# Layer 0's self attention: row maxima turned in one piece, results regrouped by DMA, the causal mask put down before the scores, and a new order of the places

## The chip, the cores and the metric

The kernel runs on one core of a Trainium2 chip. The time is the device time of one execution in microseconds (us), as the chip's profiler records it. Before the change, three runs took 2233.22, 2234.9 and 2238.18 us; their median is 2234.9 us. One more execution was taken with a full profile, and all durations below are from it. Engines are named as the profile names them: PE is TensorE doing matrix multiplications, PEld its loading of stationary operands, DVE is VectorE, ACT ScalarE, POOL GpSimd and SP SyncE, which here only issues DMAs.

## The reference

A decoder of two layers, with a layer norm behind each addition. Each layer has a self attention, a cross attention and a feed-forward part. The change touches only the first of the six, layer 0's self attention: 4 batches of 1024 positions and 256 channels, 16 heads of 16 channels, with a causal mask.

```python
def attention(x, w_in, b_in, w_out, b_out):          # x: 4 x 1024 x 256
    q, k, v = split(x @ w_in.T + b_in, 3)             # each as 16 heads of 16
    scores = einsum('bhqd,bhkd->bhqk', q / sqrt(16), k)
    scores = scores + where(tril(1024, 1024), 0, -inf)
    attn = softmax(scores, axis=-1)
    out = einsum('bhqk,bhkd->bhqd', attn, v)          # heads side by side: 4 x 1024 x 256
    return out @ w_out.T + b_out

x = layernorm(x + attention(x, ...))
... # cross attention to 154 positions, feed-forward with a convolution, then layer 1
```

The softmax is computed with the row's maximum taken off before the exponential, so each row's maximum must be known before any of its exponentials is taken.

## The kernel before

**Steps.** The self attention runs in 16 steps; step s takes batch s//4 and the four heads 4·(s%4) to 4·(s%4)+3. The four heads lie in four groups of 32 partitions: rows 0 to 15 of a group hold a head's 16 channels, row 16 is an extra one. `projected` (L275 to 289) computes queries and keys of eight heads for 512 positions at once, and `spread` (L293 to 299) moves them with four DMAs per step on SP's queue from 16 adjacent rows into their groups, `qpads` (two buffers) and `kpads` (three). Row 16 of the keys is 1.

**Two passes.** Scores are computed twice. Pass A of a step (`a_unit`) multiplies queries by keys, with queries on the partitions, only to get the row maxima on DVE: `tensor_reduce` L332 for whole blocks, L348 for blocks on the diagonal, to which the mask is first added by a matmul. `highest` (L355) joins a row's partial maxima, negated, into `nmt`, column 16 of each head's 32; `shifted_queries` (L360 to 370) turns `nmt` with eight 128x128 transposes on PE and adds it to the queries, so that row 16 of `qs` holds minus the maximum. Pass B (`b_unit`) multiplies keys by `qs`, keys on the partitions; the row of ones takes the maximum off. ACT takes the exponential (L399) into `p`, POOL zeroes what the mask forbids (L402), and `weighted` (L420 to 439) multiplies `p` with the values and sums in `acc`. The values' tile has 17 columns per head, 16 values and a one, so row 16 of a head's result is its softmax denominator. `normalised` (L441 to 455) turns the results back with eight transposes per step, takes the reciprocal of the denominators, 16 columns at a time (L454), and multiplies (L455). When a batch's four steps are done, `turned_back` (L462 to 470) transposes the normalised results once more (16 transposes per batch), and `out_projected` (L472 to 482) projects 128 positions at a time and adds `x`; the layer norm follows.

**Places.** Each pass of a step has 18 units, so a step has 18 places. At a place, `together` runs one unit of pass A of step s beside one unit of pass B of the step before (L191 is the line of the one helper that issues all these matmuls), the two in opposite pairs of row groups. A unit's product takes two of the seven PSUM banks that rotate among all that is computed here; the eighth is `acc`. Pass B of step s-1 starts two places after the step's border. In the gap between two places stands other work of PE: the products of `weighted` (a whole 512-column piece, or pieces of 384 and 128 that different gaps take), projections of later steps, transposes, output projections.

**Order.** The order of PE's work is written out by hand. Every piece is put down with a time, 20 units to a step (`at(when, ...)`, from L489 on); the pieces are sorted by that time and issued, and PE's instructions and the DMAs so marked keep that order. A piece at `s * T + 1 + j` is the pair of units of place j; pieces at `+0.5` stand in the gap behind the place before. The other engines' order follows from what PE produces.

Of the kernel before, what the change touches and what calls it, by code (L numbers as in the profile page):

```python
# [8 lines left out]
F32 = mybir.dt.float32  # L9
# [20 lines left out]
def decoder_kernel(ctx: ExitStack, tc: tile.TileContext, a: dict, out: bass.AP):  # L30
# [155 lines left out]
    def self_attention(wk, pss, psa):  # L186
# [29 lines left out]
        vts, nmps, nmts = [], [], []  # L216
        for i in range(2):
            vt = wk.tile([P, NC, 17 * H + 16], F32, tag=f"v{i}", name=f"v{i}", bufs=1)
            nc.gpsimd.memset(vt, 1.0)
            vts.append(vt)  # L220
            nmp = wk.tile([P, 4, NC, 3], F32, tag=f"nmp{i}", name=f"nmp{i}", bufs=1)
            nc.gpsimd.memset(nmp, -3.0e38)
            nmps.append(nmp)
            nmt = wk.tile([P, NC, 4, 32], F32, tag=f"nmt{i}", name=f"nmt{i}", bufs=1)
            nc.gpsimd.memset(nmt, 0.0)
            nmts.append(nmt)

        bo2 = wk.tile([P, E], F32, tag="bo2", name="bo2", bufs=1)
        t = bank()
        for e in range(2):  # L230
            mm(t[:, :E], l0a_bv[:, e : e + 1].to_broadcast([P, P]), l0a_wo[:, e, :], e == 0, e == 1)
        nc.vector.tensor_tensor(bo2, t[:, :E], l0a_bo, ALU.add)
# [6 lines left out]
        xTs, ons, sts, qss, pts, accs, ots = {}, {}, {}, {}, {}, {}, {}  # L239
# [18 lines left out]
        def values(b, i):  # L258
            t = bank()
            for j in range(2):  # L260
                c = 2 * i + j
                for e in range(2):
                    mm(
                        t[:, j * E : (j + 1) * E],
                        xTs[b][:, e, c * P : (c + 1) * P],
                        l0a_w[:, e, 2 * E :],
                        e == 0,
                        e == 1,
                    )
            (nc.vector.tensor_copy, nc.scalar.copy)[i % 2](  # L270
                vts[b % 2][:, 2 * i : 2 * i + 2, : 17 * H].rearrange("p c (h r) -> p c h r", r=17)[:, :, :, 0:16],
                t.rearrange("p (c h d) -> p c h d", c=2, h=H),
            )

        def projected(kind, i, q):  # L275
# [4 lines left out]
            t = bank()  # L280
            for e in range(2):
                mm(
                    t,
                    l0a_w[:, e, w0 + h * P : w0 + (h + 1) * P],
                    xTs[b][:, e, q * 512 : (q + 1) * 512],
                    e == 0,
                    e == 1,
                )
            nc.scalar.activation(
                sts[kind, i][:, q * 512 : (q + 1) * 512], t, AF.Identity, bias=bias[:, h : h + 1], scale=scale  # L290
            )

        def spread(kind, s):  # L293
            pads = {"k": kpads, "q": qpads}[kind]
            pad = pads[s % len(pads)]
            st = sts[kind, s // 2]
            for g in range(4):
                r = 64 * (s % 2) + 16 * g
                pe(nc.sync.dma_start(out=pad[32 * g : 32 * g + 16, :], in_=st[r : r + 16, :]))
# [12 lines left out]
        def a_unit(s, u, pair):  # L312

            t = [bank() for _ in range(2)]
# [20 lines left out]
            else:  # L335
                q0 = 4 * (u - 7)
                for j in range(4):
                    cols = slice((q0 + j) * P, (q0 + j + 1) * P)
                    rounds.append([
                        (t[g][:, j * P : (j + 1) * P], qt[rows[g], cols], kt[rows[g], cols], j == 0, False)  # L340
# [3 lines left out]
                def after():  # L344
                    for g in range(2):
                        mm(t[g], ident_bf, cmask4.rearrange("p j n -> p (j n)"), False, True)
# [8 lines left out]
        def highest(s):  # L355
            nc.vector.tensor_reduce(
                nmts[s % 2][:, :, :, 16], nmps[s % 2].rearrange("p g q i -> p q g i"), AX.X, ALU.max, negate=True
            )

        def shifted_queries(s):  # L360
            nmt = nmts[s % 2]
            qs = qss[s] = wk.tile([P, S], F32, tag="qs", name="qs")
            for q in range(2):
                t = bank()
# [1295 lines left out]
```

## Time and profile before

| what | us |
|---|---|
| median of three runs | 2234.9 |
| the profiled execution's own time | 2231.4 |
| its span in the profile | 2229.6 |
| start to the first product of pass B (step 0, pass A alone) | 0 to 69.1 |
| both passes, steps 1 to 15 | 69.1 to 702.7 |
| last step's pass B alone | 702.7 to 740.5 |
| output projection of the last batch, until the next part begins | 740.5 to 761.0 |
| all that follows (the other five parts, not touched) | 761.0 to 2229.6 |

PE is busy 94% of the span, DVE 67%, ACT 50%, POOL 23%; the mean granted clock of TensorE is 0.979 of full speed. In the stretch where both passes run, a step takes 633.6/15 = 42.2 us.

How the lines are to be read. A line of the timeline gives a start, a duration, the engine, the source line, the operation, output<-input by the program's names, the shapes, and x with the number of instructions in the group; brackets hold the idle time ahead of the group and what ended it. Matmuls are pipelined, so a group's duration overlaps with the next group's; what a group costs is the distance from its start to the start of the next one. A line of the groups gives busy time in all and the mean of one in ns, then the idle time ahead and its enders. A line of the windows gives, for one stretch, busy us and number of instructions of PE, PEld, DVE, ACT and POOL, then the granted clock, the share of time that the DMA engines were busy, and GB/s.

### The profile page before, as it was taken

The numbers are of one execution on the slowest core, as the hardware profiler recorded it, in microseconds if no ns is written. First come the engines' busy times: TensorE is split into PE (matmuls) and PEld (weight loads), VectorE is DVE, ScalarE is ACT, GpSimd is POOL, SyncE is SP. The second block draws the span as 40 slices with busy tenths as digits, with TensorE's granted clock in tenths as the row PEclk, the third lists the DMA queues.
The fourth block names the chain that finished last, engine by engine and source line by source line (L and its number), as shares of the span: only waits on it lengthen the run. The fifth ranks groups of instructions, "written<-read, shape, count | busy, mean of one in ns | idle before, by whom it ended". The sixth has DMA issues, their size and how long they took to land.

```text
span 2229.6 us, 39020 instructions
## 1 busy us (share of the span) xinstructions
PE 2100.6 (94%) x14708; PEld 1255.9 (56%) x14708; DVE 1491.3 (67%) x3287; ACT 1119.0 (50%) x2861; POOL 510.4 (23%) x1113
## 2 busy tenths in 40 slices
PE   7999999999999899989899989989999999999996
PEld 4554554555454456556556556656666655565654
DVE  4766667776775556658997888886972465555644
ACT  1455554554555365556666655554543234545444
POOL 1111111111111265445455443000000111111102
PEclk9999999999999999999999999999999999999998
DMA  4101100000000100000000100000000010010101
GB/s 111 39 6 53 37 9 15 11 16 15 6 16 1 39 1 20 1 1 1 1 1 1 34 1 22 1 0 1 1 1 1 2 20 15 15 29 10 29 1 38
DMA packets 24445, 34.85 MB, mean 16 GB/s; under 512 B 5953, under 2 KB 19649, under 8 KB 24257
## 3 DMA queue, kind: packets, MB, share of 16 engines
q1 hardware_dynamic: 22640, 31.20, 6.1%
q8 instruction: 117, 1.92, 0.4%
q10 hardware_dynamic: 1616, 1.16, 0.2%
q14 instruction: 72, 0.58, 0.1%
HBM read 15.56 MB, written 4.19 MB: 9 GB/s over the span
## 4 chain that ended last, share of the span: by engine, by line
PE 71%; DVE 20%; ACT 6%; issue 1%; POOL 1%; DMA 1%; SPq 0%; ACTq 0%; POOLq 0%; DVEq 0%
PE s L191 21%; PE t L590 15%; PE s L1196 10%; PE s L590 8%; PE acc L191 6%; DVE gt L946 4%; PE acc L1196 3%; PE t L774 2%; ACT u L749 2%; DVE nmp L332 2%; DVE x L169 1%; DVE nmx L745 1%; DVE bnst L136 1%; DVE gt L956 1%; DVE ht L932 1%
## 5 line engine op out<-in xcount | busy, mean ns | idle before, releaser
L399 ACT ACTIVATE p<-s 128x512 f32<-128x512 f32 x576 | 312.2, 595 | 291.9 <-PE s L191 283.7
L332 DVE TENSOR_REDUCE nmp<-s 128x1 f32<-128x512 f32 (+3 forms) x640 | 298.6, 522 | 153.8 <-PE s L191 153.0
L191 PE MATMUL s<-qs,kp 32*128 32x512 f32 (+3 forms) x1536 | 347.9, 521 | 0.0
L191 PE MATMUL s<-kp,qp 32*128 32x128 f32 (+3 forms) x2304 | 327.7, 407 | 2.4 <-DMA qp<-sq 2.1
L757 POOL TENSOR_SCALAR p<-u,rs 128x128 f32<-128x128 f32 x512 | 215.9, 441 | 284.8 <-DVE rs L753 185.0
L191 PEld LDWEIGHTS s<-kp,qp 32*128 32x128 f32 x2304 | 165.5, 189 | 136.1 <-ACT p L399 46.2
L402 POOL TENSOR_SCALAR_AFFINE_SELECT p<-p 128x256 f32<-128x256 f32 x256 | 99.6, 407 | 567.8 <-ACT p L399 567.8
L749 ACT ACTIVATE u<-s,nmx 128x154 f32<-128x154 f32 x512 | 192.9, 393 | 46.7 <-DVE nmx L745 30.6
L154 POOL TENSOR_TENSOR rstd<-ve,neghalf 128x4 f32<-128x4 f32 (+1 forms) x56 | 58.6, 1046 | 573.6 <-DVE ve L152 569.2
L191 PE MATMUL acc<-p,v 128*32 128x384 f32 (+3 forms) x2016 | 167.9, 420 | 0.1
L191 PEld LDWEIGHTS s<-qs,kp 32*128 32x128 f32 x1536 | 138.8, 183 | 29.1 <-DVE nmp L332 8.4
L590 PE MATMUL t<-xT,xw 128*128 128x512 f32 x256 | 123.3, 605 | 11.8 <-DVE xT L677 8.4
L1353 DVE TENSOR_REDUCE nmt<-s 128x3 f32<-128x462 f32 (+1 forms) x192 | 99.0, 578 | 45.6 <-PE s L1196 45.6
L745 DVE TENSOR_REDUCE nmx<-s 128x4 f32<-128x616 f32 x128 | 100.9, 788 | 39.5 <-PE s L590 38.2
L590 PE MATMUL t<-v,pt 128*128 128x256 f32 x512 | 116.5, 380 | 8.2 <-DVE pt L1105 8.2
L590 PE MATMUL t<-xw,ot 128*128 128x256 f32 x512 | 119.0, 387 | 2.7 <-ACT qt L731 2.6
L946 DVE SCALAR_TENSOR_TENSOR gt<-ht,cw,gt 128x256 f32<-128x256 f32 x256 | 116.4, 500 | 6.5 <-ACT gt L942 5.3
L590 PEld LDWEIGHTS s<-kt,qt 64*128 64x128 f32 x1024 | 75.9, 186 | 72.2 <-issue 50.8
L590 PE MATMUL s<-qt,xT 128*128 128x512 f32 x256 | 115.1, 592 | 0.0
L590 PEld LDWEIGHTS t<-v,pt 128*128 128x128 f32 x512 | 95.8, 190 | 30.5 <-DVE pt L1105 9.8
L348 DVE TENSOR_REDUCE nmp<-s 128x4 f32<-128x512 f32 x128 | 82.4, 686 | 44.8 <-PE s L191 44.4
L749 ACT ACTIVATION_READ_ACCUMULATOR u<-s,nmx 128x1 f32 x512 | 106.4, 208 | 0.0
(259 smaller groups left out, 3851.0 us busy)
## 6 DMA issues: line engine op xcount, KB each, us to landing
qp<-sq SPq DMA_DIRECT2D x128, 64.0 KB, 2.3
kp<-sk SPq DMA_DIRECT2D x64, 64.0 KB, 2.3
out_dram<-x SPq DMA_DIRECT2D x8, 512.0 KB, 2.9
x<-in_x_dram SPq DMA_DIRECT2D x3, 1024.0 KB, 6.5
wf<-in_L_ffn_w_dram SPq DMA_DIRECT2D x2, 1024.0 KB, 6.0
xw<-in_L_xattn_wk_dram SPq DMA_DIRECT2D x1, 1024.0 KB, 6.5
xw<-in_L_xattn_wq_dram SPq DMA_DIRECT2D x1, 1024.0 KB, 5.0
xw<-in_L_xattn_wv_dram SPq DMA_DIRECT2D x1, 1024.0 KB, 5.0
```

The costliest lines, as they stand in the source:

```text
L191: pe(nc.tensor.matmul(o, l, r, start=start, stop=stop))
L332: nc.vector.tensor_reduce(nmp[:, 2 * pair + g, qc, i : i + 1], t[g][:, c0 : c0 + n], AX.X, ALU.max)
L348: nc.vector.tensor_reduce(nmp[:, 2 * pair + g, q0 : q0 + 4, 0], t[g].rearrange("p (j n) -> p j n", j=4), AX.X, ALU.max,)
L399: nc.scalar.activation(p[:, g, :], t[g], AF.Exp)
L402: nc.gpsimd.affine_select(out=v, in_=v, compare_op=ALU.is_ge, fill=0.0, base=0, pattern=[[0, 2], [1, P]], channel_multiplier=-1,)
L590: pe(nc.tensor.matmul(o, l, r, start=start, stop=stop))
L745: nc.vector.tensor_reduce(nmx.rearrange("p i g -> p g i"), t, AX.X, ALU.max, negate=True)
L749: nc.scalar.activation(u[:, 2 * i + g, :], t[:, g, i, :], AF.Exp, bias=nmx[:, i, g : g + 1], accum_out=ssum[:, i, g : g + 1],)
L757: nc.gpsimd.tensor_scalar(p[:, h * P : (h + 1) * P], u[:, h, :P], rs[:, h : h + 1], 1.0, ALU.mult, ALU.mult)
L946: nc.vector.scalar_tensor_tensor(g, ht[:, i, k : k + N], cw[:, hc, k : k + 1], g, ALU.mult, ALU.add)
L1196: pe(nc.tensor.matmul(o, l, r, start=start, stop=stop))
L1353: nc.vector.tensor_reduce(nmts[s % 2][:, 3 * u : 3 * u + n, g, 17], ts[g][:, : n * LK].rearrange("p (c k) -> p c k", k=LK), AX.X, ALU.max, ...
```

## The change

**Maxima.** `highest` leaves the maxima as 128 positions by 32 columns (four heads by eight chunks). `maxima_turned` turns them by a single transpose into 32x128, ACT copies that out of PSUM, and four DMAs put the rows into row 16 of `qs`. `qs` itself is a copy of the queries, made by one DMA of 512 KB (`second_queries`) earlier in the step. The eight transposes and the two additions of `shifted_queries` are gone.

**Results.** The values' tile has 48 columns for a pair of heads: the values of one, 16 ones, the values of the other. A product of 32 columns then yields 16 rows of results and 16 rows that all hold the denominator. `gathered` moves both, with eight DMAs of 64 KB per step, into `on` (results, already in the form that the output projection reads) and `den` (denominators, in the same places). `divided` takes the reciprocal of `den` on DVE, all 128x128 elements of a chunk, eight chunks per pair of steps, and multiplies on POOL. The transposes of `normalised` and of `turned_back` are gone.

**Mask.** For a diagonal unit the mask is now multiplied into the bank first (`causal_mask`, start of the sum), in the gap ahead of the unit, and the scores are added to it. The diagonal units move from places 0 to 3 to places 1, 3, 5 and 7; `a_order` and `b_order` keep the two passes in opposite row groups.

**Order.** Pass B starts four places after the border, not two. Each piece of `weighted` is issued whole, in every second gap, except one piece of 256 columns, with the two of another unit beside it. Projections are made in quarters of 256 positions and values one chunk at a time. The first spread of queries is issued on ACT's queue; the bias of the output projection is computed later, not ahead of everything. For the last batch, half of its last step's results are gathered on their own and the output projection of the first four chunks is placed in the last step.

```diff
-    vt = wk.tile([P, NC, 17 * H + 16], F32, tag=f"v{i}", name=f"v{i}", bufs=1)
+    vt = wk.tile([P, NC, 24 * H], F32, tag=f"v{i}", name=f"v{i}", bufs=1)
...
+T = 20
+DELAY = 4
+
+def gap(s, j):
+    return (s + j // 18) * T + 1.5 + j % 18
...
+def values(b, c):
+    t = bank()[:, :E]
+    for e in range(2):
+        mm(t, xTs[b][:, e, c * P : (c + 1) * P], l0a_w[:, e, 2 * E :], e == 0, e == 1)
+    (nc.vector.tensor_copy, nc.scalar.copy)[c % 2](
+        vts[b % 2][:, c, :].rearrange("p (h r d) -> p h r d", r=3, d=16)[:, :, 0:3:2, :],
+        t.rearrange("p (h r d) -> p h r d", r=2, d=16),
     )
...
-    t = bank()
+    t = bank()[:, :256]
+    cols = slice(q * 256, (q + 1) * 256)
...
+    queue = nc.scalar if (kind, s) == ("q", 0) else nc.sync
     for g in range(4):
         r = 64 * (s % 2) + 16 * g
-        pe(nc.sync.dma_start(out=pad[32 * g : 32 * g + 16, :], in_=st[r : r + 16, :]))
+        pe(queue.dma_start(out=pad[32 * g : 32 * g + 16, :], in_=st[r : r + 16, :]))
+
+def second_queries(s):
+    qs = qss[s] = wk.tile([P, S], F32, tag="qs", name="qs")
+    pe(nc.sync.dma_start(out=qs, in_=qpads[s % 2]))
...
+diagonal = {1: (7, 0), 3: (7, 1), 5: (8, 0), 7: (8, 1)}
+b_order = [divmod((j - DELAY) % 18, 2) for j in range(18)]
+b_order = [(i, 1 - pair if i in (8, 1) else pair) for i, pair in b_order]
+others = [iter((4, 5, 6, 0, 1, 2, 3)) for _ in range(2)]
+a_order = []
+for j, (_, pair) in enumerate(b_order):
+    a_order.append(diagonal[j] if j in diagonal else (next(others[1 - pair]), 1 - pair))
+
+def causal_mask(s, j):
+    t = masks[s, j] = [bank() for _ in range(2)]
+    for g in range(2):
+        mm(t[g], ident_bf, cmask4.rearrange("p j n -> p (j n)"), True, False)
+
+def a_unit(s, j):
+    u, pair = a_order[j]
+    t = masks.pop((s, j)) if j in diagonal else [bank() for _ in range(2)]
...
             rounds.append([
-                (t[g][:, j * P : (j + 1) * P], qt[rows[g], cols], kt[rows[g], cols], j == 0, False)
+                (t[g][:, c * P : (c + 1) * P], qt[rows[g], cols], kt[rows[g], cols], False, c == 3)
...
-            for g in range(2):
-                mm(t[g], ident_bf, cmask4.rearrange("p j n -> p (j n)"), False, True)
...
-def shifted_queries(s):
...
+    hm = hms[s] = wk.tile([P, 4, NC], F32, tag="hm", name="hm")
+    nc.vector.tensor_reduce(hm, nmps[s % 2], AX.X, ALU.max, negate=True)
+
+def maxima_turned(s):
+    t = bank()[:32, :P]
+    pe(nc.tensor.transpose(t, hms[s].rearrange("p g c -> p (g c)"), ident))
+    rows = wk.tile([32, P], F32, tag="mrow", name="mrow")
+    nc.scalar.copy(rows, t)
+    for g in range(4):
+        pe(nc.sync.dma_start(
+            out=qss[s][32 * g + 16 : 32 * g + 17, :].rearrange("p (c n) -> p c n", c=NC),
+            in_=rows[NC * g : NC * g + NC, :],
+        ))
...
+            v0 = 24 * (4 * t4 + g) - 8 * (g % 2)
-                vts[b % 2][:, kc, 17 * (4 * t4 + g) : 17 * (4 * t4 + g) + 32],
+                vts[b % 2][:, kc, v0 : v0 + 32],
...
-def normalised(s, i):
...
-    t = bank()
-    for j in range(4):
-        c = c0 + j
-        pe(nc.tensor.transpose(t[:, j * P : (j + 1) * P], ot[:, c * P : (c + 1) * P], ident))
...
-    rs = small.tile([P, 4, 4], F32, tag="rs8", name="rs8", bufs=2)
-    nc.vector.reciprocal(rs, v[:, :, :, 16])
...
-def turned_back(b, e, q):
...
+def gathered(s, c0=0, n=S, queue=None):
     b, t4 = divmod(s, 4)
+    e = t4 // 2
+    if t4 == 0:
+        ons[b] = wk.tile([P, 2, S], F32, tag="on", name="on")
+    if t4 % 2 == 0:
+        dens[b, e] = wk.tile([P, S], F32, tag="den", name="den", bufs=1)
+    cols = slice(c0, c0 + n)
+    for g in range(4):
+        r = 64 * (t4 % 2) + 16 * g
+        up = 32 * g + 16 * (g % 2)
+        down = 32 * g + 16 * (1 - g % 2)
+        pe(nc.sync.dma_start(out=ons[b][r : r + 16, e, cols], in_=ots[s][up : up + 16, cols]))
+        pe((queue or nc.sync).dma_start(out=dens[b, e][r : r + 16, cols], in_=ots[s][down : down + 16, cols]))
+
+def divided(b, e, c0, n):
+    cols = slice(c0, c0 + n)
+    den, on = dens[b, e][:, cols], ons[b][:, e, cols]
+    nc.vector.reciprocal(den, den)
+    nc.gpsimd.tensor_tensor(on, on, den, ALU.mult)
...
-        mm(t, onT[:, e, c * P : (c + 1) * P], l0a_wo[:, e, :], e == 0, e == 1)
+        mm(t, ons[b][:, e, c * P : (c + 1) * P], l0a_wo[:, e, :], e == 0, e == 1)
...
+at(gap(0, 9), output_bias)
...
+    s0 = 4 * b
+    for q in range(2):
+        for e in range(2):
+            at(gap(s0 - 2, 2 * q) + 0.1 * e if b else -60 + 2 * q + e, x_transposed, b, e, q)
+    places = [(s0 - 1, 14), (s0 - 1, 16), (s0, 0), (s0, 2), (s0, 4), (s0, 14), (s0, 16), (s0 + 1, 0)]
+    if b == 0:
+        places[:2] = [(0, 1), (0, 3)]
+    for c, (s, j) in zip((0, 1, 3, 2, 6, 4, 5, 7), places):
+        at(gap(s, j), values, b, c)
+    places = [(s0 + 5, 14), (s0 + 5, 16), (s0 + 6, 4), (s0 + 6, 14), (s0 + 6, 16), (s0 + 7, 0), (s0 + 7, 2), (s0 + 7, 4)]
+    if b == NB - 1:
+        places[:4] = [(s0 + 4, j) for j in (14, 15, 16, 17)]
+    for c, (s, j) in enumerate(places):
+        at(gap(s, j), out_projected, b, c)
+    for e in range(2):
+        if (b, e) == (NB - 1, 1):
+            for q in range(2):
+                at(gap(s0 + 4, 12.2) if q == 0 else gap(s0 + 5, 5.5), divided, b, e, 512 * q, 512)
         else:
+            for c in range(NC):
+                at(gap(s0 + 2 * e + 3, 9.2 + c), divided, b, e, P * c, P)
...
+    for q in range(4):
+        for kind in "kq":
+            if i == 0:
+                at(-57 + q + 0.1 * (kind == "q"), projected, kind, i, q)
+            else:
+                at(gap(2 * i - (2 if kind == "k" else 1), 6 + 2 * q), projected, kind, i, q)
...
+            at(gap(s - 1, 13.1 if j == 0 else 4.1), spread, "k", s)
+            at(gap(s - 1, 13.2 if j == 0 else 2.1), spread, "q", s)
...
-    at((s + 1) * T + 1.4, shifted_queries, s)
+    at(gap(s + 1, 0) - 0.1, maxima_turned, s)
+    at(gap(s, 4.3), second_queries, s)
...
+    for i in range(9):
+        g = gap(s + 1, 2 * i + 3 + DELAY)
+        for qh, kc, c0 in b_sets[i]:
+            if (i, qh) == (2, 1):
+                continue
+            n = width(qh, kc)
+            last = (i, qh) == (2, 0) or (i, kc) == (8, 7)
+            at(g, weighted, s, qh, i, [(kc, c0, 512 - n, n)], i in (0, 3), last)
+        if i == 3:
+            at(g, weighted, s, 1, 2, [(6, 256, 256, 256)])
+    if s < 4 * NB - 1:
+        at(gap(s + 2, 5.3), gathered, s)
+    else:
+        at(gap(s + 1, 11.2), gathered, s, 0, 512, nc.scalar)
+        at(gap(s + 2, 5.3), gathered, s, 512, 512, nc.scalar)
+    for j in diagonal:
+        at(gap(s, j - 1) + 0.3, causal_mask, s, j)
...
-            units.append((a_unit, s, (7, 8, 0, 1, 2, 3, 4, 5, 6)[j // 2], 1 - j % 2))
-
+            units.append((a_unit, s, j))
+        sb = s - 1 if j >= DELAY else s - 2
         if 0 <= sb < 4 * NB:
-            units.append((b_unit, sb, jb // 2, jb % 2))
+            units.append((b_unit, sb, *b_order[j]))
```

## The prediction

> **What bounds the kernel now.** I read the page's busy shares first, then windows by stage, then PE's timeline over one step with DVE's beside it, then the groups by form, and last the DMA issues. The stages (PE, PEld, DVE, ACT, POOL, clock, DMA share, GB/s), from the windows:
>
> ```profile
> 0.00:69.10 69.10, 52.29 (x272) 32.85 (x272) 36.91 (x76) 7.75 (x11) 7.22 (x16) 0.87 0.36 93
> 69.10:702.70 633.60, 628.47 (x6145) 324.34 (x6144) 439.22 (x952) 336.64 (x615) 96.76 (x241) 1.00 0.09 19
> 702.70:740.50 37.80, 34.76 (x294) 15.40 (x292) 12.91 (x36) 22.53 (x43) 8.78 (x21) 1.00 0.01 2
> 740.50:761.00 20.50, 12.16 (x72) 10.69 (x72) 17.24 (x55) 2.70 (x6) 6.67 (x9) 0.93 0.30 103
> ```
>
> In the 633.6 us with both passes PE is busy 628.5, DVE 439. Two kinds of time are inside PE's: work, and waits too short to show, because a matmul in flight counts as busy. PE's timeline (start, duration) prices the work and shows such waits:
>
> ```profile
> 374.88 1.06 PE L191 MATMUL acc<-p,v 128*32 128x512 f32 x8
> ...
> 382.03 1.98 PE L191 MATMUL s<-xT,qkv 128*128 128x512 f32 x4
> 383.94 0.70 PE L191 MATMUL s<-kp,qp 32*128 32x512 f32 x2
> ...
> 386.90 1.13 PE L191 MATMUL s<-wo,onT 128*128 128x256 f32 x4
> 387.96 0.64 PE L191 MATMUL acc<-p,v 128*32 128x256 f32 x8
> 388.53 0.70 PE L191 MATMUL s<-kp,qp 32*128 32x512 f32 x2
> ...
> 406.55 1.07 PE L366 MATMUL s<-ident,nmt 128*128 128x128 f32 x8 [0.52 <-DVE nmt L356]
> 407.45 0.60 PE L451 MATMUL s<-ident,ot 128*128 128x128 f32 x4
> 407.99 0.38 PE L191 MATMUL s<-kp,qp 32*128 32x128 f32 x2
> ...
> 416.85 0.66 PE L451 MATMUL s<-ident,ot 128*128 128x128 f32 x4
> 417.44 0.70 PE L191 MATMUL s<-kp,qp 32*128 32x512 f32 x2
> ...
> 418.10 1.30 PE L191 MATMUL s<-qs,kp 32*128 32x384 f32 x7
> 419.33 0.85 PE L191 MATMUL acc<-p,v 128*32 128x384 f32 x8
> ```
>
> From start to next start: nmt and ot transposes 407.99-406.55 = 1.44 a step, four transposes 0.59, a 512-column projection of two banks 1.91, an output chunk 1.06, a 256-column piece of `acc` 0.57. Equal distances give 1.00, 0.78, 0.36 for 512, 384, 128 columns: 0.143 + 0.2135 per 128. A place's pair of units takes 1.08.
>
> The hidden wait is at 417.44: this pair takes 1.89. Its second half starts at 418.10, where DVE has just (418.22) cleared the two banks of the unit before:
>
> ```profile
> 416.93 1.29 DVE L332 TENSOR_REDUCE nmp<-s 128x1 f32<-128x512 f32 x2 [0.98 <-PE s L191]
> ```
>
> So PE's work sets the pace, but seven banks couple it to DVE: a gap of only 0.59 between two units costs 0.8 of waiting. Some 40 such gaps make about 30 us.
>
> **The change, part by part.** The base is the profiled execution's own time, 2231.4 us (span 2229.6 and 1.8 around it), 3.5 under the median of the three runs.
>
> *1. PE's work, on the path.* Transposes removed from the stretch 69 to 740: 16 of 1.44, 16 of 0.59 (second half of ot) and 12 of 0.59 (turned back, three batches), 39.5. Added: 16 turns of the maxima at 0.27, worked out as a quarter of 1.07; bounds 0.11 (one transpose's distance in 407.45 to 407.99, with the rest hidden) and 0.59 (a group of four), so 2 to 9 us in all; 4.3. Pieces of `acc` fall from 206 to 143: 63 starts of 0.143, -9. Projections in quarters: 52 of 1.06 for 26 of 1.91, +5.5; values one by one, 24 for 12 in the same way, +3; four output chunks come over from the tail, +4.2; the 64 mask products stay, at distances of 0.44 to 0.53, of which I take about a third at the lower one instead of the higher, -2. Together -35.2-9+10.7, taken as -34.
>
> *2. Bank waits.* Now 30. Afterwards the alternate gaps hold one piece of at least 1.06, and at places 8, 10, 12, 14, 16 the second half of pass B takes the banks that the preceding unit's reductions free 0.08+1.29 = 1.37 after its end: 0.31 of wait each, 0.5 behind a split unit, 1.74 a step, 28; some 5 for the other places. +3 net. Bounds: none of these waits is left (-30), or each is the 0.8 seen at 417.44 (rival C).
>
> *3. The reciprocals: DVE, in front of the reductions that PE waits for.* `divided` puts eight 128x128 reciprocals into the step behind each pair of steps. In the built order they stand on DVE at places 8 to 12 of seven steps: one, then three, three and one between pairs of reductions. No row shows 128 columns. The rows with fewer (groups: busy, mean ns | idle before):
>
> ```profile
> L753 DVE RECIPROCAL rs<-ssum 128x4 f32<-128x4 f32 x128 | 22.1, 173 | 49.6 <-ACT u L749 44.9 <-POOL p L757 2.7 <-issue 1.2
> L857 DVE RECIPROCAL sc<-am 128x8 f32<-128x8 f32 x4 | 0.8, 194 | 0.0
> L454 DVE RECIPROCAL rs<-s 128x16 f32<-128x16 f32 x32 | 7.9, 248 | 10.1 <-PE s L451 10.1
> L332 DVE TENSOR_REDUCE nmp<-s 128x1 f32<-128x128 f32 x128 | 35.9, 280 | 9.8 <-PE s L191 9.8
> ```
>
> A single column takes 162 ns (another group), so an element costs (248-162)/15 = 5.7 ns and 128 columns 248+112x5.7 = 0.89 us. Ends: 0.28, if a long one runs as the reduction of 128; 1.0, by the steepest pair of rows (54 ns for 8 elements). Counted from the end of place 8's unit, with R for one reciprocal: place 9's reductions end at 4.05; three reciprocals and place 10's reductions end at 5.33+3R, which place 11's second half waits for; three more, place 11's reductions, one more and place 12's end at 7.89+7R; place 13 ends 1.08 later, at 8.97+7R in place of 11.2. The loss is 7R-2.2, 4.0 a time and +28 for seven. At R = 0.28 it is 0, at 1.0 33. POOL's multiplication (0.44 for 128x128, 97 of 634 us busy) and the removed additions of L370 (0.68, two a step) and L454/L455 are beside PE.
>
> [...]
>
> *4. Gathering.* SP issues eight more DMAs a step, in program order, behind place 5. Spread DMAs are the nearest:
>
> ```profile
> 437.65 2.41 SPq L299 DMA_DIRECT2D qp<-sq  x4
> qp<-sq SPq DMA_DIRECT2D x128, 64.0 KB, 2.3
> ```
>
> Four of them start within 2.41, 0.63 apart; 2.3 is the landing. From the end of `acc`: ACT's copy 0.75, seven distances of 0.63 up to the last of eight issues 4.4, landing 2.3: 7.45. DVE comes to the first reciprocal at 7.3. So it waits about 0.15, +1 in seven steps; the queue's other entries (spreads, maxima) are places apart. There is no slack (rival B). If the eight go out as slowly as the slowest spread issues, 1.59 apart, it is late by 6.7.
>
> *5. Maxima.* `maxima_turned` is in the place of the transposes, and PE waits for `highest` as now (0.52 at 406.55). Then ACT's copy (0.3, as a 128-column reduction), four issues 2.5, landing 2.3, queue and semaphores: about 8.0 behind pass A's end; pass B's first unit, moved from the second to the fourth place, comes at 10.6. The cover is the four places, 2.6 us; cost 0. The 512 KB copy of the queries is issued 14 places earlier; it lands in 2.9, as the output's 512 KB rows. At worst, rival D.
>
> *6. Ends.* Head: values and the output bias leave the start and queries spread on ACT's queue, so the first unit, at 30.67 behind a DMA, could start at about 26.4; two more places run pass A alone (+2.2), and the start has fewer groups at half clock: -7 (0 to -12). Step 16: the first output chunk at gap 14 needs copy, four issues, landing, a reciprocal of 512 (four of 128: 3.6) and a multiplication, 9.6, of which 4.65 are covered: +5 (3 to 7). Tail: 20.5 becomes 19.7, as DVE's 17.2 of additions and norms there is the limit and only half moves: -1.
>
> Sum: -34+3+28+1+0-7+5-1 = -5, **2226 us**. Against the median, all the same, it would be 2230. With 0.2%, 4.5 us, as the bound of what a measurement tells from no change, it is at the edge of faster.
>
> **The rivals.**
>
> *A: reciprocals as fast as plain operations.* Then R = 0.28, part 3 is 0: 2226-28 = 2198. Against it, the three rows grow steadily with columns. For it, none has more than 16, and start-up may be in the growth.
>
> *B, the slower side: results land late.* The gather's eight issues are the only ones of that length in a row. If they go 1.0 apart (median 0.58, longest 1.59), the last is 3 late and DVE, whose queue is in order, holds the reductions behind the reciprocal; PE stops within two places. 3x7 = 21: 2247. From 1.5 us of lateness on the kernel is slower than before by over 0.2%.
>
> *C: bank waits of 0.8 everywhere.* If a gap of 1.06 gives B no more relief than one of 0.59 does, five places x16x0.8 = 64 for 33: 2257. For it, DVE gains work at exactly those places; against it, pairs behind two-bank gaps of 1.0 now take 1.08.
>
> *D: pass B waits for the maxima's DMAs.* Each us over the 2.6 of cover counts 16 times; one over gives 2242. Against it: it needs 8.0 to become 11.6.
>
> **How the numbers follow.** Main case 0.45, A 0.17, B 0.20, C 0.12, D 0.06. The main case's own range is 2212 to 2238: R between 0.74 and 1.0 (-7, +5), bank waits half or up by a fifth (-10, +6), ends. Over all the range is 2198 to 2251: it goes from the middle of A past B and D, and leaves C's larger half. Faster: half of the main case and all but a little of A, 0.41; same: a third of the main case, 0.14; slower: the rest of it and B, C, D, 0.45.
>
> **What would show it.** Rows of L366, L451's and L467's transposes gone, 16 transposes to 32x128 in their place; `acc` groups 143; first unit of pass A near 26; 128x128 reciprocals of 0.89; at places 10 to 13 of odd steps about 4 us more than in even ones, PE's wait put down to DVE `nmp`. A DVE wait on a DMA of `den` speaks for B, waits of 0.8 in even steps for C, a PE wait on `qs` rows at the fourth place for D. Wrong altogether would be a unit that no longer takes 1.08, or copies into row 16 that slow other transfers.

## The result

The changed kernel is slower: a median of 2252.7 us over five runs (2250.3 to 2261.7) against 2234.9 for the kernel before; the ratio is 1.0086, with a 95% interval of 1.0062 to 1.0109. The forecast was 2226 with a range up to 2251, so its likeliest case lay on the wrong side and the result just outside the range. The profiled execution took 2250.3 us, with a span of 2248.0 against 2229.6.

The windows of the changed kernel, cut at the places that answer to the four windows of before (first product of pass B, end of pass A, last product of `acc`, next part's first copy); columns as before:

```profile
0.00:73.40 73.40, 56.77 (x300) 37.89 (x303) 37.47 (x82) 9.89 (x20) 6.72 (x14) 0.84 0.33 92
73.40:702.00 628.60, 617.09 (x5514) 306.71 (x5513) 455.74 (x949) 333.91 (x644) 122.86 (x296) 1.00 0.20 44
702.00:753.50 51.50, 44.14 (x275) 15.63 (x274) 13.47 (x29) 24.76 (x48) 11.05 (x24) 0.77 0.09 17
753.50:776.60 23.10, 8.52 (x44) 7.07 (x40) 13.90 (x28) 1.37 (x3) 6.19 (x9) 0.71 0.31 103
```

The last step is what stands out: pass B alone took 37.8 us and takes 51.5, at a mean clock of 0.77 where it was 1.00. For all that follows, the two traces and those of the experiments are divided by PE's own events into four stretches: to the turning of step 1's maxima ("head"), from there to the turning of step 15's ("14 steps"), on to the first product of the next part ("last step and tail"), and the rest.

| us | head | 14 steps | last step and tail | rest | span |
|---|---|---|---|---|---|
| before | 104.1 | 601.1 | 56.6 | 1467.9 | 2229.6 |
| after | 104.4 | 599.6 | 73.3 | 1470.7 | 2248.0 |
| difference | +0.3 | -1.5 | +16.7 | +2.8 | +18.4 |

So the bulk of the change, 14 steps with all their transposes, DMAs and reciprocals, came out nearly even, as the sum had it. The time was lost where only pass B runs. PE's timeline there:

```profile
703.00 1.13 PE L191 MATMUL s<-qs,kp 32*128 32x512 f32 x4
...
718.00 1.35 PE L191 MATMUL s<-qs,kp 32*128 32x512 f32 x8
721.16 1.90 PE L191 MATMUL acc<-p,v 128*32 128x512 f32 x16 [1.81 <-ACT ot L447]
722.99 2.08 PE L191 MATMUL s<-qs,kp 32*128 32x512 f32 x4
725.00 1.22 PE L191 MATMUL s<-wo,on 128*128 128x256 f32 x2
730.22 1.22 PE L191 MATMUL s<-wo,on 128*128 128x256 f32 x2 [4.00 <-POOL on L469]
731.38 2.08 PE L191 MATMUL s<-qs,kp 32*128 32x512 f32 x4
733.38 2.08 PE L191 MATMUL s<-wo,on 128*128 128x256 f32 x4
...
763.30 3.99 PE L191 MATMUL s<-wo,on 128*128 128x256 f32 x10 [9.10 <-POOL on L469]
```

Two waits stand in it. At 721.16 `acc` cannot be cleared, because ACT's copy out of it waits: `ot`, the tile that the copy writes, has a single buffer (the kernel before had two), and the gather of step 14 still reads it. At 730.22 the second half of the first output chunk, the channels of the batch's last two steps, waits for its divided results. From 722.1 on the same work also takes almost twice as long: four matmuls of a unit last 2.08, where they lasted 1.13 at 703.00. The clock by windows, and the two long reciprocals on DVE that the output chunks wait behind:

```profile
704.10:722.10 18.00, 15.56 (x155) 6.14 (x157) 0.00 (x0) 15.09 (x30) 6.24 (x16) 1.00 0.18 32
722.10:746.00 23.90, 19.90 (x56) 7.04 (x52) 9.58 (x18) 4.94 (x9) 1.26 (x1) 0.50 0.05 12
746.00:753.50 7.50, 6.58 (x65) 1.94 (x57) 2.95 (x9) 4.13 (x8) 3.54 (x7) 1.00 0.00 0
```

```profile
725.47 3.35 DVE L468 RECIPROCAL den<-den 128x512 f32<-128x512 f32 x1 [22.49 <-DMA den<-ot]
...
758.54 3.35 DVE L468 RECIPROCAL den<-den 128x512 f32<-128x512 f32 x1 [8.33 <-DMA den<-ot]
```

PE is busy 19.9 of the 23.9 us at half clock; half of that, 10 us, is my estimate of the loss. The step's account: 10 for the clock, 1.8 and 4.0 for the two waits, 4 for output chunks that came over from the tail, which makes 20. Against it stand some 3 us of transposes that are gone and some 3 us of batch 2's output chunks (three of them) that now come earlier, so that from the turning of step 15's maxima to the last product of `acc` PE takes 49.4 instead of 35.4. The tail did not get shorter (21.5 before, 24.1 after, from the last product of `acc` on), since its second half now waits 9.1 for gather, reciprocal and multiplication.

### The profile page after: what moved, and what is told of

Read it like the earlier page. It is cut to its first block, busy times and chain, and to the rows that moved or that the text cites. A ratio compares the mean times of both kernels' runs of the same rounds, so it can differ in the third digit from the quotient of the medians.

```text
span 2248.0 us, 38049 instructions
## 1 busy us (share of the span) xinstructions
PE 2101.9 (93%) x14051; PEld 1241.8 (55%) x14052; DVE 1505.7 (67%) x3257; ACT 1119.0 (50%) x2901; POOL 538.6 (24%) x1169
## 4 chain that ended last, share of the span: by engine, by line
PE 66%; DVE 22%; ACT 6%; issue 2%; DMA 1%; SPq 1%; POOL 1%; ACTq 0%; POOLq 0%; DVEq 0%
PE s L191 20%; PE t L598 15%; PE s L1204 10%; PE s L598 7%; PE acc L191 5%; DVE gt L954 4%; PE acc L1204 3%; DVE den L468 2%; DVE nmp L343 2%; ACT u L757 2%; PE t L782 2%; DVE x L169 1%; DVE nmx L753 1%; DVE gt L964 1%; DVE ht L940 1%
## 5 line engine op out<-in xcount | busy, mean ns | idle before, releaser
L191 PE MATMUL s<-qs,kp 32*128 32x512 f32 (+3 forms) x1536 | 372.4, 527 | 8.1 <-DVE nmp L343 8.0
L191 PE MATMUL s<-kp,qp 32*128 32x128 f32 (+3 forms) x2304 | 332.5, 407 | 5.5 <-DMA qp<-sq 5.4
L191 PEld LDWEIGHTS s<-qs,kp 32*128 32x128 f32 x1536 | 151.1, 185 | 55.2 <-DVE nmp L343 34.9
L191 PE MATMUL acc<-p,v 128*32 128x512 f32 (+3 forms) x1536 | 156.1, 499 | 3.4 <-ACT ot L447 1.8
L757 ACT ACTIVATION_READ_ACCUMULATOR u<-s,nmx 128x1 f32 x512 | 106.4, 208 | 0.0
```

The costliest lines, as they stand in the source:

```text
L191: pe(nc.tensor.matmul(o, l, r, start=start, stop=stop))
L757: nc.scalar.activation(u[:, 2 * i + g, :], t[:, g, i, :], AF.Exp, bias=nmx[:, i, g : g + 1], accum_out=ssum[:, i, g : g + 1],)
```

## The experiments

Each single execution carries its own pauses at half clock, so the tables' stretches are compared, not only the time. "Half clock" is how long the clock's record stood at 0.5 in the stretch named. "After" is the changed kernel's profiled execution.

### Four runs on the reciprocals and the last step

Without the short reciprocals:

```diff
-            nc.vector.reciprocal(den, den)
+            if n > P:
+                nc.vector.reciprocal(den, den)
```

> Leaves out the 56 reciprocals of 128x128 (the results are multiplied by the denominators instead); the two of 512 columns stay, and so does every transfer and wait. Theory of the bursts: each of the seven odd steps from 3 to 15 loses 4.0 us to three reciprocals standing between reductions, so these steps become about 4 us shorter, the even ones stay, and the profiled time falls from 2250.3 by 28 to about 2222. Rival (the reciprocals fit beside PE's work, and the steps are long for the bank waits alone): steps 3 to 15 stay within 0.5 us each, the time within 5 us of 2250.

The last batch's output chunks all at the end:

```diff
             if b == NB - 1:
-                places[:4] = [(s0 + 4, j) for j in (14, 15, 16, 17)]
+                places = [(s0 + 6, j) for j in range(NC)]
```

> The last batch's first four output chunks go behind pass B, with the other four; the wait of 4.0 us for them inside the last step is gone, the wait of 1.8 us of acc for the copy out of it (single buffer ot, held by the gather of the step before) stays. Theory W (the half clock from 722 to 746 us comes of the 1.8 us wait): the clock still falls to 0.5 near 722, some 10 us of half clock remain, the time falls by 4 to 7, to 2243 to 2246. Theory L (it takes the 4.0 us wait): the clock stays at 1.00 through pass B's end, the last step ends about 13 us earlier, 2237.

A buffer of its own for the last step's results:

```diff
-                    ots[s] = wk.tile([P, S], F32, tag="ot", name="ot", bufs=1)
+                    ots[s] = wk.tile([P, S], F32, tag="sk" if s == 4 * NB - 1 else "ot", name="ot", bufs=1)
```

> The last step's results get a buffer of their own (the one of the projected keys, idle by then), so acc no longer waits 1.8 us for the gather of step 14; the first output chunks stay inside the last step. Theory W: the clock is 1.00 until the wait for the first output chunk, which PE reaches about 2 us sooner and so waits at least 4 us for; the half clock then starts there, and the gain is 2 to 6 us, 2244 to 2248. Theory L: the same start of the half clock, gain 2. A rival, that this wait is the whole cause: the wait at the output chunk shrinks too, since the copy, the gather and the reciprocal all start earlier, the clock stays at 1.00, and the gain is 12 or more, under 2238.

And both of these edits together:

> Both edits. If the loss behind the last maxima (16.8 us more than before up to the next part's first product) comes of these two waits and the half clock that follows them, it goes down to about 3 us: pass B alone takes 35 us at full clock as before, the end 24 us. The time falls by about 14, to 2236. If pass B alone is slow for another reason (POOL's masking, or transfers), more than 8 of the 16.8 us stay and the time stays above 2242.

| us | time | head | 14 steps | half clock in them | last step and tail | half clock in it |
|---|---|---|---|---|---|---|
| after | 2250.3 | 104.4 | 599.6 | 3.4 | 73.3 | 38.2 |
| no reciprocals | 2224.0 | 104.4 | 573.8 | 0 | 73.8 | 38.7 |
| late output | 2245.5 | 105.4 | 613.5 | 44.4 | 55.3 | 8.6 |
| second `ot` | 2257.1 | 104.0 | 610.3 | 30.6 | 68.9 | 22.7 |
| both | 2244.4 | 109.1 | 605.4 | 17.1 | 55.9 | 9.3 |

*The reciprocals cost 25.8 us*, 28 expected: the seven odd steps lose 3.0 to 4.3 each (step 3: 44.0 with them, 39.9 without), the even ones nothing. Less than 2 us of it belong to the 3.4 us at half clock in step 15. One burst on DVE in the changed kernel, and what PE does meanwhile:

```profile
164.77 1.35 DVE L343 TENSOR_REDUCE nmp<-s 128x1 f32<-128x128 f32 x4
166.03 2.56 DVE L468 RECIPROCAL den<-den 128x128 f32<-128x128 f32 x3
168.52 1.22 DVE L343 TENSOR_REDUCE nmp<-s 128x1 f32<-128x512 f32 x2
169.65 2.56 DVE L468 RECIPROCAL den<-den 128x128 f32<-128x128 f32 x3
172.14 1.22 DVE L343 TENSOR_REDUCE nmp<-s 128x1 f32<-128x512 f32 x2
```

```profile
167.62 1.13 PE L191 MATMUL s<-kp,qp 32*128 32x512 f32 x4
169.20 1.71 PE L191 MATMUL s<-qs,kp 32*128 32x512 f32 x4 [0.45 <-DVE nmp L343]
170.84 0.64 PE L191 MATMUL acc<-p,v 128*32 128x256 f32 x8
```

One, three, three, one, as the built order had it. Pass A's half of the unit starts at 167.62; pass B's half needs the banks of the pair before and starts at 169.20, as the first of the two reductions ends that stood behind three reciprocals (168.52, 0.61 each). PE's idle row (0.45) shows only the end of that stall.

*The last step* is settled by the late output: 73.3 falls to 55.3, and to 55.9 with both edits, a little under before's 56.6, and pass B alone runs at full clock. What starts the half clock is not settled. In the run with late output the wait of 1.8 for `ot` was still there, and no half clock followed it; in the changed kernel and in the run without reciprocals 23.9 us at half clock began right behind the same wait and ahead of the one for the output chunk. So neither theory W nor theory L holds as written. What all runs with output chunks inside the last step have is a wait of 4 to 6 us there and 22.7 us or more of half clock in the stretch; the runs without have 13 us or less, here and below. A second `ot` alone gains 4.4 of the 16.7, with the wait at the output chunk grown to 6.1 and the half clock starting only there; the rival that the buffer is the whole cause is out.

*Late output should have brought 13 us and brought 5*: the last stretch gained 18, but the 14 steps lost 14, without an edit in them. The windows of that run say how, first around the burst of step 3, then in the last step:

```profile
168.00:172.00 4.00, 3.55 (x12) 1.24 (x10) 4.00 (x7) 1.32 (x3) 1.60 (x4) 0.97 0.00 0
172.00:182.20 10.20, 10.20 (x45) 3.50 (x44) 5.74 (x9) 4.04 (x8) 1.58 (x4) 0.51 0.17 28
182.20:192.00 9.80, 9.80 (x70) 3.91 (x66) 5.74 (x10) 4.61 (x9) 0.00 (x0) 1.00 0.32 107
...
719.00:750.00 31.00, 27.30 (x249) 9.79 (x248) 3.35 (x1) 24.10 (x48) 9.79 (x23) 1.00 0.15 28
```

Behind a burst, where PE had idled less than half a microsecond by the record, the clock fell to half for 10.2 us while PE was busy all the time. (The record shows only the end of such a stall: the pair of units there takes 3.32 from start to next start, where 1.42 is usual.) Of the seven bursts, five were followed by half clock in this run: three by 10.2 us (from 171.8, 260.5 and 438.0), one by 6.8 (from 530.2), the last by twice 3.4. In the profiled run of the changed kernel only the last was, by 3.4 us. The steps in question are 1.6 to 3.6 us longer (step 3: 47.5 instead of 44.0), 14 together. The runs without bursts, the one without reciprocals and all that follow, had none in the 14 steps. So the bursts cost 26 us by waiting, and up to 14 more that differ from run to run. Half clock also accounts for most of two more misses: second `ot` took 2257.1, not 2244 to 2248, with 14 steps 10.7 longer than after's, and both edits 2244.4, not 2236, with 14 steps 5.8 and a head 4.7 longer.

### Reciprocals one at a time, the head, and the size of the bank waits

One reciprocal per place, with the reductions and reciprocals held in the written order on DVE (this and all later versions keep the two edits of the last step):

```diff
-                        at(gap(s0 + 2 * e + 3, 9.2 + c), divided, b, e, P * c, P)
+                        at(gap(s0 + 2 * e + 3, (9, 10, 12, 13, 15, 16, 19, 21)[c]) + 0.2, divided, b, e, P * c, P)
...
-            nc.vector.reciprocal(den, den)
+            pe(nc.vector.reciprocal(den, den))
...
-                            nc.vector.tensor_reduce(
+                            pe(nc.vector.tensor_reduce(
```

> The two edits of the end stay in; the eight reciprocals of a pair of steps no longer stand in a burst but one at a time, behind the reductions of places 9, 10, 12, 13, 15, 16 and, in the next step, 1 and 3, with the reductions held in that order. A place has about 2.1 us with its gap, a pair of reductions 1.29 and a reciprocal 0.92, so DVE just keeps up. Theory of the bursts: most of the 26 us that leaving the reciprocals out saved come back, and the pauses at half clock that follow bursts (10 us long, none without reciprocals) go with them: steps 3 to 15 within 1 us of those without reciprocals, the time 2218 to 2224. Rival (it is DVE's load, not the order): each reciprocal goes on costing 0.46 us wherever it stands, and the time stays at 2238 to 2243.

Then also the head:

```diff
-                at(gap(s, j), values, b, c)
+                at(-53 + 0.1 * c if b == 0 and c < 4 else gap(s, j), values, b, c)
...
-        at(gap(0, 9), output_bias)
+        at(-52, output_bias)
```

> As the spread reciprocals, and the first four chunks of values and the output bias go ahead of the first unit, where PE idles 5.4 us for the spread queries and keys. Theory: the work (five groups, 2.1 us each at half clock) fills that wait, and pass A of step 0 has five groups fewer; the first maxima are turned 5 to 7 us earlier than at 68.7, the stretch at half clock from 26 to 43 us is shorter, and the time is about 6 lower than that of the spread reciprocals alone, 2212 to 2218, 0.7 to 1.0% under before. Rival (the spread transfers, not PE, set the start of every early unit): the first maxima stay within 2 us and so does the time.

And the halved reductions, on the kernel without reciprocals and on the kernel before:

```diff
-                                nmp[:, 2 * pair + g, qc, i : i + 1], t[g][:, c0 : c0 + n], AX.X, ALU.max
+                                nmp[:, 2 * pair + g, qc, i : i + 1], t[g][:, c0 : c0 + n // 2], AX.X, ALU.max
...
-                            nmp[:, 2 * pair + g, q0 : q0 + 4, 0], t[g].rearrange("p (j n) -> p j n", j=4),
+                            nmp[:, 2 * pair + g, q0 : q0 + 4, 0], t[g].rearrange("p (j n) -> p j n", j=4)[:, :, : P // 2],
```

> On the kernel without the 56 reciprocals, each reduction of pass A reads only the first half of its columns, so the maxima are those of half the scores; DVE frees a pair of banks about 0.5 us earlier. The step that this tests is the bank waits, put at 33 us for the changed kernel (0.31 behind each two-bank gap of 1.06). If that size holds, PE's waits vanish and the time falls from 2224 by 25 to 33, to 2191 to 2199. If the waits are mostly gone already (0 was the lower bound) it stays above 2216; if they are 0.8 each (64 us) it falls under 2175.

> The same halved reductions in the kernel before. The bank waits were put at 30 us there, some 40 gaps of 0.59 with 0.8 of waiting each; with reductions of about 0.83 a pair instead of 1.29, 0.3 of each 0.8 should be left, and the time falls by 16 to 22, from 2229 to about 2210. If the waits of before are smaller than I read them, it falls by less than 10; if other gaps wait too, by more than 28.

| us | time | head | 14 steps | last step and tail |
|---|---|---|---|---|
| spread reciprocals | 2216.1 | 104.5 | 580.3 | 55.9 |
| spread and head | 2209.1 (2206.8 to 2215.2) | 99.0 | 580.3 | 56.1 |
| no reciprocals, half maxima | 2184.0 | 97.3 | 547.1 | 69.6 |
| before, half maxima | 2201.0 | 97.3 | 579.0 | 56.6 |

*Spreading* brings 19 of the 26 us back (599.6 to 580.3; without any reciprocal 573.8), and no half clock in the 14 steps. It is the order on DVE that costs, not the load: the 56 reciprocals are as long as before or a little longer (940 ns instead of 918). DVE in step 3, from the version with the head moved as well:

```profile
160.33 1.29 DVE L343 TENSOR_REDUCE nmp<-s 128x1 f32<-128x512 f32 x2
161.53 0.94 DVE L468 RECIPROCAL den<-den 128x128 f32<-128x128 f32 x1
162.46 1.29 DVE L343 TENSOR_REDUCE nmp<-s 128x1 f32<-128x512 f32 x2
164.45 1.29 DVE L343 TENSOR_REDUCE nmp<-s 128x1 f32<-128x512 f32 x2 [0.70 <-PE s L191]
165.65 0.94 DVE L468 RECIPROCAL den<-den 128x128 f32<-128x128 f32 x1
```

*The bank waits* had the right size. PE's timeline shows them place by place. In step 8 of the changed kernel, where DVE has no reciprocals, the pairs of units at places 8, 10, 12, 14 and 16 take 1.56, 1.42, 1.42, 1.42 and 1.42 from start to next start, all others 1.07 to 1.09; with halved reductions all take 1.07 to 1.09. Place 10, first in the changed kernel, then in the run without reciprocals and with halved reductions:

```profile
386.04 0.70 PE L191 MATMUL s<-kp,qp 32*128 32x512 f32 x2
...
387.46 0.64 PE L191 MATMUL acc<-p,v 128*32 128x256 f32 x8
```

```profile
355.77 0.70 PE L191 MATMUL s<-kp,qp 32*128 32x512 f32 x2
...
356.84 0.64 PE L191 MATMUL acc<-p,v 128*32 128x256 f32 x8
```

These waits make 1.89 us a step, where the prediction had 1.74. Halving the reductions takes 26.7 us off the 14 steps behind the change (573.8 to 547.1), 25 to 33 expected, though heads gain as well and the time falls by 40; in the kernel before it takes 22.0 (601.1 to 579.0), at the upper end of 16 to 22, and there it does not remove every wait: in one step a pair of 1.89 becomes 1.36. All units and masks of the 14 steps, the same work in both kernels, take 335.0 us before and 343.3 in the changed kernel without reciprocals (313.1 and 316.0 with halved reductions). So the waits grew by about 8, where the prediction had 3. In the kernel before, 5 of the 22 stand at the units with a mask behind them (94.3 us with their masks, 89.2 with halved reductions), where I had looked only at the gaps of 0.59. The 11 that one of the expectations below gives for them is too much: the halved run's trace lacks 27 of some 110 mask products, and their time falls to the unit ahead.

*The head* is not settled. The profiled run with it had its second maxima 5.5 us earlier than the run without, but the first maxima, which the expectation was about, only 0.8; the repetition below had the second ones at 106.4. What differs is how long the clock stands at half around the first units: 13.7 us there, 27.3 in the repetition, 17 to 20 in most runs of the old head. Taking half of that time off leaves, as an estimate, 92 to 93 for the new head and 94 to 96 for the old and for before, some 2 us of gain.

### The parts undone one by one

From the version with spread reciprocals and moved head, one part of the change at a time is put back as it was. The maxima by transposes (the columns of `nmt` are packed more tightly than before to fit, 112 instead of 128 to a chunk, so that one row of the queries picks up a neighbour's maximum; the work is the same):

```diff
-            pe(nc.tensor.transpose(t, hms[s].rearrange("p g c -> p (g c)"), ident))
...
+            for q in range(2):
+                t = bank()
+                for j in range(4):
+                    c = 4 * q + j
+                    pe(nc.tensor.transpose(t[:, j * P : (j + 1) * P], nmt[:, 112 * c : 112 * c + P], ident))
+                cols = slice(q * 512, (q + 1) * 512)
+                nc.vector.tensor_tensor(qs[:, cols], t, qpads[s % 2][:, cols], ALU.add)
```

> On the version with spread reciprocals and the moved head (2209), the maxima are turned as before again: eight transposes and two additions, no copy of the queries by DMA and no DMAs into row 16. Measured distances say 0.83 for the eight transposes beside four others, up to 1.07 alone, against 0.12 for the single one: 0.7 to 0.95 a step on PE. If DVE's 1.36 of additions per step stay beside PE's work, 16 steps cost 11 to 15 and the time is 2220 to 2224; if the additions delay the reductions of the first places one for one, up to 37 and 2246. Rival: the new way's DMAs cost somewhere what the transposes did; then the time stays within 4 of 2209.

The mask behind the scores:

```diff
-            t = masks.pop((s, j)) if j in diagonal else [bank() for _ in range(2)]
+            t = [bank() for _ in range(2)]
...
                 def after():
+                    for g in range(2):
+                        mm(t[g], ident_bf, cmask4.rearrange("p j n -> p (j n)"), False, True)
                     for g in range(2):
...
-                at(gap(s, j - 1) + 0.3, causal_mask, s, j)
```

> On the same version, the mask's products go behind the diagonal unit's scores again, so the unit's banks are reduced 0.5 us later, and nothing else moves. In the kernel before, halving the reductions took 11 us off the distances behind masks, so a wait stands there. Theory: the later reductions are waited for at two or three of the four diagonal places, 0.3 to 0.5 each, in 16 steps 10 to 30 us: 2219 to 2239. Rival: PE's other pieces in those gaps cover it, and the time stays within 4 of 2209.

The results by transposes, with `normalised` and `turned_back` as in the kernel before:

```diff
-                at(gap(s + 2, 5.3), gathered, s)
...
+            for i in range(2):
+                at(gap(s + 2, 6 * i), normalised, s, i)
...
+                at(gap(s0 + 5, 8 + 2 * i if b < NB - 1 else 6.1 + 0.1 * i), turned_back, b, e, q)
```

> On the same version, the results are turned back by transposes again (two groups of four per step, four groups per batch), with reciprocals of 16 columns and the old layout of the values; no gathering DMAs, no 128-column reciprocals. PE gets 2x0.59 a step and 2.35 a batch, 28 us in all; what goes are the 6.6 us that spread reciprocals still cost over 14 steps, and 3 us at the end (a gather, a reciprocal of 512 and a multiplication ahead of the last output chunks). So 15 to 22 more, 2224 to 2231. If groups of 0.59 bring their waits of 0.8 with them as at 417.44 in the trace of before, up to 25 more than that. Rival, that gathering is worth nothing when its reciprocals are counted: within 5 of 2209.

And the version itself again:

> The version that the three are compared with, on their chip, with more rounds: 2206 to 2215, a ratio of 0.988 to 0.994 to before. Between executions the difference should lie in pauses at half clock near the head and the last step, not in steps 2 to 15.

| us | time | head | half clock in it from about the first unit on | 14 steps | last step and tail |
|---|---|---|---|---|---|
| spread and head, again | 2213.1 (2210.6 to 2215.7) | 106.4 | 27.3 | 580.4 | 56.1 |
| maxima undone | 2221.6 | 106.8 | 27.3 | 588.1 | 56.3 |
| mask undone | 2218.4 | 97.0 | 10.2 | 593.2 | 57.6 |
| gather undone | 2219.1 | 106.4 | 27.3 | 587.4 | 55.2 |

The run with the mask undone had a short pause in the head, so its time understates what that costs; by the 14 steps, free of half clock in all four, *the mask first is worth 12.8 us, the maxima 7.7, the gather 7.0*. The mask was in the range expected (10 to 30 in all); the maxima came under (11 to 15). The gather came out at a third of the 15 to 22: four transposes cost less than I had charged. In this run they stand beside other pieces:

```profile
415.07 0.60 PE L459 MATMUL s<-ident,ot 128*128 128x128 f32 x4
415.51 0.59 PE L191 MATMUL s<-cmask,ident_bf 128*128 128x512 bf16 x2
...
419.19 0.66 PE L475 MATMUL s<-ident,on 128*128 128x128 f32 x4
419.69 1.03 PE L191 MATMUL s<-xT,qkv 128*128 128x256 f32 x4
```

0.44 and 0.50 from start to start, not 0.59, in all about 18 us; and leaving the spread reciprocals out takes 10 off the units' distances. The two ends of the account are near each other, which is why the reciprocals' place decides over the whole part.

The version with spread reciprocals and moved head beats both kernels: ratios to before of 0.9906 (0.9876 to 0.9937) and 0.9915 (0.9893 to 0.9936). Its repetition kept to the expected range except for one execution at 2215.7, whose head stood 27.3 us at half clock from about the first unit on; the 14 steps were 580.3 and 580.4.

## Why the prediction was wrong

*Steps 1 to 5 held.* Their sum was -34+3+28+1 = -2 us; the 14 steps give -1.5. Singly: transposes went from 41.8 to 7.1 us of PE's distances (-34.7; I had -35.2 for all 16 steps), the single one costs 0.13, an eighth of the row of eight, where I took a quarter, 0.27:

```profile
403.17 0.28 PE L370 MATMUL s<-ident,hm 128*32 128x128 f32 x1
403.30 1.03 PE L191 MATMUL s<-qkv,xT 128*128 128x256 f32 x4
```

`acc` -7.9 (-9), projections and values +5.1 (+8.5 for all 16 steps and the start), output chunks +1.7 in these steps. The reciprocals' length, 0.89 by extrapolation from at most 16 columns, is 0.918, and the walk through places 8 to 12 gave 4.0 a burst where 3.0 to 4.3 were measured. Rival A is out. The account closes: -36 of work, +8 on units and masks (bank waits, 3 in the sum) and +26 of reciprocals are -2.

```profile
L468 DVE RECIPROCAL den<-den 128x128 f32<-128x128 f32 x56 | 49.0, 918 | 4.8 <-POOL p L409 2.2 <-DMA on<-ot 1.4 <-DMA den<-ot 1.0
L468 DVE RECIPROCAL den<-den 128x512 f32<-128x512 f32 x2 | 6.7, 3353 | 30.8 <-DMA den<-ot 30.8
```

The same rows answer rival B: in front of 56 reciprocals DVE waited 2.4 us for gathering DMAs in all. Rival D did not come either; in the 14 steps PE has no wait on a DMA. Rival C's 0.8 at five places isn't there: they show 0.35 to 0.5. An element, put at 5.7 ns from at most 16 columns, costs (3353-918)/384 = 6.3 ns between 128 and 512 columns by the two rows.

*Step 6, the ends, failed*; with 2.8 us in the next part it makes 23 of the 24 us between 2226 and 2250.3. Head, -7 forecast, +0.3: the first unit did start earlier (28.4 for 30.7), but I counted the values' work as gone when it had moved from a wait for DMAs, where it was free, in between the units: projections, values and (after the change) the output bias between the first unit and the turning of the first maxima take 8.3 us before and 15.1 after. At 26.4 I had also put the first unit 2 us too early. Last step, +5: "the first output chunk at gap 14 needs copy, four issues, landing, a reciprocal of 512 (four of 128: 3.6) and a multiplication, 9.6, of which 4.65 are covered" was right as a wait (4.0), but it is not the whole cost. I missed that the change leaves `ot` a single buffer. Its reader, the gather, is covered in ordinary steps: in step 9, 15.5 us pass from its first issue to the next copy into `ot` (415.48 to 431.01). In the last step PE was there after 7.1 (712.23 to 719.35), ahead of the landing, and the copy came at 720.46. And I had no term for the clock in this step, though the windows of before showed 0.87 in the head and 0.93 in the tail. Tail, -1: "DVE's 17.2 of additions and norms there is the limit and only half moves" overlooked that the other half now waits 9.1 behind its own gather and reciprocal; it became 2.6 longer. The remaining 2.8 lie in the next part, around whose start the clock stands at half for 10.2 us; it stood so for 6.8 in the kernel before, and for 6.8 with late output, with a second `ot` and with both, so it isn't put down to the change.

The rivals were all about the 16 steps; the case that came was in none of them. The slower side had its 0.45 for other reasons, so that part of the forecast was right by luck. The chance of faster was also added up a little too high: half of the main case's 0.45 and A's 0.17 are 0.395, not 0.41.

## What to carry to other kernels

Price the places where cover ends (first step, last step, tail) as carefully as the steady state: a buffer or a chain that is covered in every full step may not be in the last one, and work that is free inside a wait isn't once it is moved out. Look at the clock beside PE's waits: the last step of the changed kernel had 5.8 us of waits and 23.9 us at half clock, an estimated loss of 10 more, and such pauses differed between runs of the same code (3.4 or 44.4 us in the 14 steps). When work is added to an engine that frees another's buffers, its place in that engine's order can count more than its length: the same 56 reciprocals cost 26 us in bursts of three and 7 spread out.

## What the runs showed of the hardware

All pauses at half clock in the profiled runs lasted a multiple of 3.4 us: 3.4, 6.8, 10.2, 13.7, 17.1, 23.9 or 27.3, but for the one that a profile's end breaks off. They are not the same from run to run. The same code had 3.4 or 44.4 us of them in its 14 steps, and the same head 13.7 or 27.3. The clock also stood at half while PE was busy: in the run with late output PE was busy by the record in all of 172.0 to 182.2, 10.2 us at a mean clock of 0.51; in the changed kernel the clock stood at half for 23.9 us (722.1 to 746.0), with PE busy 19.9 of them and one wait of 4.0 us inside.

A reciprocal on DVE took 0.918 us for 128 columns and 3.353 for 512 in the changed kernel, 6.3 ns an element between the two, where a reduction of 512 took 0.68.
